# Where a recurrent block's scan states are emitted, its preparation in whole pieces, and a causal mask over one tile of keys

## The chip, the cores and the metric

The kernel runs on one core of a Trainium2 chip. The core has five engines that work side by side from queues of their own: TensorE (PE, matrix products; its weight loads are listed as PEld), VectorE (DVE), ScalarE (ACT, elementwise functions), GpSimd (POOL) and SyncE (SP, which issues the transfers). The metric is the device time of one execution in microseconds (us).

## The reference

The reference is a decoder of four layers over x of shape (4, 256, 256), that is 1024 tokens of width 256, with a context ctx_1024 of shape (4, 256, 128). Each layer has three parts, and each part is added and normalised, with a layernorm over the 256 features. The first five parts are the ones that matter here.

```python
x = _layernorm(x + _L0_attn_ref(x, ...))             # causal attention, 16 heads, one key/value head
x = _layernorm(x + _L0_xattn_ref(ctx_1024, x, ...))  # selective scan over the context, gated by x
x = _layernorm(x + _L0_ffn_ref(x, ...))              # "thought": 4 recurrent steps on the last token
x = _layernorm(x + _L1_attn_ref(x, ...))             # attention, 16 heads of 16, 4 key/value heads
x = _layernorm(x + _L1_xattn_ref(ctx_1024, x, ...))  # a second selective scan
...                                                  # experts and two more layers
```

The first attention masks keys above the diagonal before the softmax:

```python
sim = jnp.einsum('bhid,bjd->bhij', q, k)             # 16 heads of 128, rope on q and k
sim = jnp.where(jnp.triu(jnp.ones((n, n), dtype=bool), 1), neg, sim)
attn = jax.nn.softmax(sim - jnp.max(sim, axis=-1, keepdims=True), axis=-1)
```

The scans depend on the context alone, until the gate at their end:

```python
u = jax.nn.silu(xc + conv_b[None, :, None])          # xc: projection and 4-tap convolution
delta = jax.nn.softplus(jnp.einsum('er,brl->bel', dt_proj_w, dt_lo) + dt_proj_b[None, :, None])
dA = jnp.exp(d_t[..., None] * A)                     # 256 channels x 16 states
state = state * dA + (d_t * u_t)[..., None] * B_t[:, None, :]
y_t = jnp.einsum('ben,bn->be', state, C_t)
y = (y + D[None, :, None] * u) * jax.nn.silu(z)      # z is x
```

The thought's four steps form one dependent chain; what follows them covers all tokens:

```python
thought = x_norm[:, -1, :] @ agg_w + agg_b
for _ in range(4):
    t = jax.nn.gelu(layer_norm(thought, pn_gamma, pn_beta) @ d1_w + d1_b)
    thought = thought + (t @ d2_w + d2_b)
out = x + jax.nn.sigmoid(x @ gate_w + gate_b) * (thought @ bc_w + bc_b)[:, None, :]
return layer_norm(out, out_gamma, out_beta)
```

## The kernel before, in words

The 1024 tokens lie in 8 tiles of 128 partitions. x stays on the chip, with a transposed copy xT for the products. The parts run one after another; the two scans have no place of their own, but are pieces of work that other parts emit among their own instructions. Every helper of class `Core` (lines 45 to 215) issues one instruction: `K.mm` a matrix product (L132), `K.tt`, `K.ts`, `K.stt` on VectorE (L111 to L120), `K.ptt` on GpSimd (L123), `K.act` on ScalarE (L126), `K.reduce` a row maximum or sum on VectorE (L129). Most instructions therefore show the line of a helper and are told apart by their tiles. A scheduler puts each engine's instructions into an order of its own by priorities that follow the order of emission, so that the place where a piece of work is emitted moves it on the engines' queues, but does not fix it there.

**The first attention** (`run_mqa`, L232 to L395) loops over n from 0 to 31: batch n // 8, four heads, and tile t = n % 2 of that batch's two query tiles. The keys that such a tile may see are ns = 128 for even n and 256 for odd n. `queries` (L281) makes the rotated queries of two heads for a whole batch, one call for each n. `scores` (L297) fills one PSUM bank for two heads: a mask product in bf16 comes first and opens the accumulation (L307), then one f32 product for each head. The mask tile maskb is 256 wide, its first half zeros and its second the triangle; for odd n the mask product covers all 256 keys of both heads, 512 columns, of which the first 128 of each head add zeros. VectorE then takes the row maxima, ScalarE the exponentials p; `shares` scales them by the reciprocal sums, `turn` transposes them into pT, `sums` and `output` multiply by values and output weights. The first scan is begun ahead of the loop (`K.scans.begin("l0x")`), and every n emits two of its states (`K.scans.beside(2)`).

**A scan** (`Scans._steps`, L443) begins with a preparation. From the context it makes u (Silu), then delta and du: VectorE writes delta = product + bias (L481), ScalarE writes du = Abs of the same (L482), in four pieces of 512 each. Then softplus is put together as max(delta, 0) + Ln(1 + Exp(-|delta|)): Exp and Ln (L484 to L486) each run over the two channel chunks of 1024, and two VectorE operations for each chunk (L487 to L489) finish delta and du = delta times u. A state is one step of the loop over 4 batches and 16 states: SP's queue loads B and C for it into bc (256 KB, L515), ScalarE makes dA with two Exps, VectorE forms s = du times B, scans along the tokens (L522), multiplies by C, and two states later TensorE adds s into a PSUM bank (ssmps). bc and s have four buffers, dA three. `beside(n)` emits the next n states; a scan has 64.

**Thought** (`run_thought`, L645 to L788) begins the second scan (`K.scans.begin("l1x")`, L714) ahead of its four steps. A step is a chain: square, variance product, root on GpSimd, scale, the product with d1, Gelu, a transposition with the copy hT on ScalarE (L740), the product with d2, the copy add on ScalarE (L744) and the next ct. The gate's products fill in, and one Sigmoid makes all eight gates. After the fourth step thT is ready (L760), and there 24 states are emitted (L761). The tail follows: for each batch `gated` multiplies the gate by the broadcast thought and adds x, with moments on VectorE and a root on GpSimd; `added` normalises, adds and calls `settle`, which normalises again and transposes x into xT.

**The second attention** (`run_gqa`, from L997) makes query, key and value projections for 8 tiles, rotates them on VectorE and transposes them, with one state beside each tile, and then emits one state beside each of its 32 rounds: 24 + 8 + 32 are the second scan's 64 states.

Of the kernel before, what the change touches and what calls it, by code (L numbers as in the profile page):

```python
# [20 lines left out]
BF16 = mybir.dt.bfloat16  # L21
# [3 lines left out]
AF = mybir.ActivationFunctionType  # L25
# [6 lines left out]
P = 128  # L32
B, L, D = 4, 256, 256
NT = B * L // P
DC = D // P
# [170 lines left out]
def again(ap, n):  # L206

    return ap.unsqueeze(1).to_broadcast([ap.shape[0], n, ap.shape[1]])
# [23 lines left out]
def run_mqa(K, w, more):  # L232
    nc, tc = K.nc, K.tc
    with ExitStack() as ctx:
        one = ctx.enter_context(tc.tile_pool(name="mqa1", bufs=1))
# [7 lines left out]
        mask = one.tile([P, P], F32, name="mask")  # L243
# [2 lines left out]
            out=mask, in_=mask, compare_op=ALU.is_ge, fill=NEG, base=0, pattern=[[-1, P]], channel_multiplier=1  # L246
        )

        maskb = one.tile([P, 2 * P], BF16, name="maskb")
        nc.gpsimd.memset(maskb[:, 0:P], 0.0)  # L250
        nc.vector.tensor_copy(maskb[:, P : 2 * P], mask)
        rope = w["rope"]

        def rotated(out, ps, cos, sin):
# [9 lines left out]
        kT = one.tile([P, B * L], F32, name="kT")  # L264
# [32 lines left out]
        def scores(n):  # L297
            b, g, t = n // 8, n // 2 % 4, n % 2
            ns = P * (t + 1)
            p = wk.tile([P, 4, L], F32, name="p")  # L300
            nm = wk.tile([P, 4], F32, name="nm")
            sm = wk.tile([P, 4], F32, name="sm")
            for jj in range(2):
                q = qT[8 * b + 2 * g + jj]
                sc = psc.tile([P, 2, L], F32, name="sc", tag="sc")

                K.mm(sc[:, :, 0:ns], K.identb, again(maskb[:, 2 * P - ns :], 2), True, False)  # L307
                for j in range(2):
                    K.mm(sc[:, j, 0:ns], q[:, j, t * P : (t + 1) * P], kT[:, b * L : b * L + ns], False, j == 1)
                two = slice(2 * jj, 2 * jj + 2)  # L310
                K.reduce(nm[:, two], sc[:, :, 0:ns], MAX, negate=True)
                for j in range(2):
                    m = 2 * jj + j
                    K.act(p[:, m, 0:ns], sc[:, j, 0:ns], AF.Exp, bias=nm[:, m : m + 1], accum_out=sm[:, m : m + 1])
            made[n] = p, sm
# [46 lines left out]
        queries(1)  # L362
        values(0)
        scores(0)
        rest = [lambda: values(1), lambda: keys(1), lambda: values(2), lambda: values(3)]
        for n in (2, 3):
            queries(n)
        for n in range(N):
            shares(n)
            if n + 1 < N:  # L370
                scores(n + 1)
            if n + 4 < N:
                queries(n + 4)
            if n in (2, 3, 4, 5):
                rest.pop(0)()
            if n == 6:
                ready = ready_thought(K, more()) if K.fused(0) else iter(())
            if n > 9:
                next(ready, None)
            K.scans.beside(2)  # L380
            turn(n)
            if n:
                output(n - 1)
            sums(n)
            if n % 8 == 2 and n > 8 and K.fused(0):
                gate_pair(K, wk, y, n // 8 - 1)
# [12 lines left out]
class Scans:  # L399
# [43 lines left out]
    def _steps(self, pre):  # L443
        K, nc, w, wk = self.K, self.K.nc, self.w[pre], self.wk
# [4 lines left out]
        du = self.one.tile([P, DC, N], F32, name="du")  # L449
# [3 lines left out]
        for j in range(4):  # L453
            t = wk.tile([P, D], F32, name="tap", tag="bc", padded_shape=[P, 2 * L])
# [14 lines left out]
        for h in range(2):  # L469
# [8 lines left out]
            for c in range(DC):  # L478
# [2 lines left out]

                K.ts(delta[:, c, s], ps, cols[:, c, 1:2], None, ADD)  # L482
                K.act(du[:, c, s], ps, AF.Abs, bias=cols[:, c, 1:2])
        for func, kw in ((AF.Exp, dict(scale=-1.0)), (AF.Ln, dict(bias=K.eps[1.0]))):  # L484
            for c in range(DC):
                K.act(du[:, c, :], du[:, c, :], func, **kw)  # L486
        for c in range(DC):  # L487
            K.stt(delta[:, c, :], delta[:, c, :], 0.0, du[:, c, :], MAX, ADD)
            K.tt(du[:, c, :], delta[:, c, :], u[:, c, :], MUL)  # L489
# [18 lines left out]
        for b in range(B):  # L508
            lo = b * L
            for n in range(16):  # L510
# [3 lines left out]
                t = wk.tile([P, 2, L], F32, name="bc", tag="bc")  # L514
# [130 lines left out]
def run_thought(K, w, more):  # L645
    nc, tc = K.nc, K.tc
# [3 lines left out]
    with ExitStack() as ctx:  # L650
        one = ctx.enter_context(tc.tile_pool(name="th1", bufs=1))
# [106 lines left out]
        nc.vector.tensor_copy(mean, last)  # L758
        thT = wk.tile([P, DC, B], F32, name="thT")
        K.tt(thT, ct, again(mean, DC), ADD)  # L760
        K.scans.beside(24)  # L761

        def gated(b):

            ps = pm.tile([P, D], F32, name="ps", tag="mm")
            K.mm(ps, K.ident, row["bc_b"], True, False)
            for c in range(DC):
                K.mm(ps, thT[:, c, b : b + 1].to_broadcast([P, P]), w["bc"][:, c, :], False, c == DC - 1)
            for i in (2 * b, 2 * b + 1):
                K.tt(gate[:, i, :], gate[:, i, :], ps, MUL)  # L770
                K.tt(gate[:, i, :], gate[:, i, :], K.x[:, i, :], ADD)
                K.ptt(K.x[:, i, :], K.x[:, i, :], row["out_b"], ADD)
            return moments(gate[:, 2 * b : 2 * b + 2, :], P, 2)

        def added(b, mv, rstd):
            for t in range(2):
                i = 2 * b + t
                g = gate[:, i, :]
                K.stt(g, g, mv[:, t, 0:1], row["out_g"], SUB, MUL)
                K.stt(K.x[:, i, :], g, rstd[:, t : t + 1], K.x[:, i, :], MUL, ADD)  # L780
                K.settle(i)

        ahead = gated(0)
        for b in range(B):
            this = ahead
            if b + 1 < B:
                ahead = gated(b + 1)
            added(b, *this)  # L788

# [1441 lines left out]
def load_none(K, wp):  # L2233
    return {}


PARTS = [
    (load_mqa, run_mqa),
    (load_none, run_gate("l0x")),
    (load_thought, run_thought),  # L2240
    (load_gqa, run_gqa),
    (load_none, run_gate("l1x")),
# [210 lines left out]
```

## Time and profile before

| | |
|---|---|
| median of three runs | 2461.66 us (2461.66, 2462.14, 2454.41) |
| profiled execution, its own time | 2449.13 us |
| its span, first to last instruction | 2447.4 us |
| mean granted clock of TensorE | 0.952 |
| instructions | 28725 |
| PE busy | 2259.7 us (92%) |
| PEld busy | 1516.4 us (62%) |
| DVE busy | 1472.1 us (60%) |
| ACT busy | 808.9 us (33%) |
| POOL busy | 257.9 us (11%) |
| mask products | 64, of them 32 with 512 columns |
| scan states | 128, mean 1218 ns for the scan itself |

The profile is that of one execution. It gives, for each engine, the time busy; the span in 40 equal slices, where a digit is the busy share in tenths and PEclk the clock that the throttle granted to TensorE, in tenths of full speed; and groups of instructions. The trace behind it answers with timelines. A line of a timeline has the start and the duration in us, the engine, the line in the kernel, the operation, the tile written and the tiles read with their shapes, how many such instructions were folded into one line (x4), and in brackets the idle time ahead of it with the instruction that ended it. Neighbours on one engine overlap a little in these records, so that the distance between two starts is the better price of the first.

### The profile page before, as it was taken

Reading aid. Unit: us, or ns where it says so; the run is one execution under the profiler, and the core shown is the slowest. Engines: PE = TensorE matmul, PEld = TensorE weight load, DVE = VectorE, ACT = ScalarE, POOL = GpSimd, SP = SyncE. Lnnn points to the kernel's source line nnn. Section 1 sums busy time; section 2 is a strip of 40 time slices with the busy share of each in tenths; the row PEclk is TensorE's granted clock in tenths of the full one; section 3 lists DMA queues with packets and bytes.
Section 4 is the critical chain, followed back from the end, with each engine's and each line's share of the span. In section 5 each row is a group of like instructions: output and inputs, shape, how many; then the busy total and the mean of one; then the engine's idle time right before and its main releaser. Section 6 shows DMA issues by size and latency. Waiting matters only on the chain. (4 is left out here: it accounts for less than half of the span.)

```text
span 2447.4 us, 28725 instructions
## 1 busy us (share of the span) xinstructions
PE 2259.7 (92%) x10632; PEld 1516.4 (62%) x10632; DVE 1472.1 (60%) x3002; ACT 808.9 (33%) x1803; POOL 257.9 (11%) x422
## 2 busy tenths in 40 slices
PE   8899997769996999899999999999999988899997
PEld 4566763334433655537888888888776543476774
DVE  4899984989976121370465444454655676773566
ACT  5677665413441111261211111111113243343434
POOL 0000001030010322200110001100210003000001
PEclk9899998778988999999999999999989899999999
DMA  6222221412213644220131111110100002100000
GB/s 204 63 59 60 52 56 33 103 27 52 48 31 101 192 129 123 76 68 14 65 108 61 46 66 53 63 46 31 47 22 1 20 18 71 41 1 1 1 1 18
DMA packets 132834, 138.98 MB, mean 57 GB/s; under 512 B 13876, under 2 KB 120726, under 8 KB 130904
## 3 DMA queue, kind: packets, MB, share of 16 engines
q1 hardware_dynamic: 132696, 137.16, 19.5%
q8 instruction: 84, 1.38, 0.2%
q14 instruction: 54, 0.44, 0.1%
HBM read 134.27 MB, written 2.85 MB: 56 GB/s over the span
## 5 line engine op out<-in xcount | busy, mean ns | idle before, releaser
L132 PE MATMUL ps<-xw,xcT 128*128 128x256 f32 (+1 forms) x2304 | 518.9, 382 | 0.3 <-ACT YT L126 0.3
L132 PEld LDWEIGHTS ps<-xw,xcT 128*128 128x128 f32 x2304 | 430.8, 190 | 64.0 <-issue 1.9
L132 PE MATMUL sc<-kT,qT 32*128 32x256 f32 (+2 forms) x1024 | 240.4, 402 | 10.6 <-DVE qn L129 10.3
L132 PEld LDWEIGHTS sc<-kT,qT 128*128 128x128 f32 (+1 forms) x1024 | 152.0, 200 | 94.1 <-issue 59.5
L111 DVE TENSOR_TENSOR xp<-ps,xb 128x256 f32<-128x256 f32 x96 | 40.4, 421 | 231.7 <-PE ps L132 231.7
L126 ACT ACTIVATE dA<-delta,negA 128x255 f32<-128x255 f32 x256 | 119.0, 501 | 144.3 <-DVE s L522 142.7
L132 PE MATMUL ssmps<-s,idz 128*128 128x512 f32 x256 | 146.2, 680 | 16.5 <-DVE s L111 14.7
L522 DVE TENSOR_TENSOR_SCAN s<-dA,s 128x512 f32<-128x512 f32 x128 | 154.5, 1218 | 2.6
L111 DVE TENSOR_TENSOR hT<-u,a 128x512 f32<-128x512 f32 x48 | 33.1, 690 | 184.0 <-PE u L132 184.0
L126 ACT ACTIVATE p<-sc,nm 128x256 f32<-128x256 f32 (+1 forms) x256 | 111.9, 444 | 94.1 <-DVE nm L129 88.0
L126 ACT ACTIVATE sq<-xp 128x1024 f32<-128x1024 f32 x24 | 25.4, 1057 | 314.3 <-DVE xp L111 314.2
L132 PE MATMUL o<-pT,vt 128*128 128x256 f32 (+1 forms) x352 | 116.9, 453 | 9.8 <-ACT pT L332 9.4
L129 DVE TENSOR_REDUCE qn<-sc 128x2 f32<-128x480 f32 (+1 forms) x192 | 87.1, 506 | 40.5 <-PE sc L132 40.0
L169 POOL TENSOR_SCALAR rstd<-mv 128x2 f32<-128x2 f32 x48 | 11.6, 241 | 944.9 <-DVE mv L161 935.1
L126 ACT ACTIVATE e<-sT 128x512 f32<-128x512 f32 x128 | 70.9, 590 | 106.7 <-PE sT L132 105.6
L132 PE MATMUL sT<-q,kT 32*128 32x256 f32 (+1 forms) x384 | 101.5, 505 | 3.5 <-ACT e L126 3.3
L1489 DVE TENSOR_TENSOR_SCAN dec<-xT,idz 128x256 f32<-128x256 f32 (+1 forms) x192 | 89.8, 536 | 20.3 <-DMA xT<-ad 20.3
L129 DVE TENSOR_REDUCE nm<-sc 128x2 f32<-128x512 f32 (+1 forms) x128 | 77.3, 613 | 40.8 <-PE sc L132 40.3
L126 ACT ACTIVATE a<-g 128x512 f32<-128x512 f32 x48 | 28.8, 599 | 206.2 <-PE g L132 203.4
L132 PE MATMUL g<-xT,wj 128*128 128x512 f32 x192 | 90.3, 593 | 0.7 <-ACT rows L100 0.7
L132 PE MATMUL u<-xT,wj 128*128 128x512 f32 x192 | 90.4, 592 | 0.0
L111 DVE TENSOR_TENSOR s<-du,bc 128x512 f32<-128x512 f32 x128 | 87.6, 694 | 4.4 <-PE ssmps L132 2.4
(502 smaller groups left out, 3950.9 us busy)
## 6 DMA issues: line engine op xcount, KB each, us to landing
bc<-bcd SPq DMA_DIRECT2D x128, 256.0 KB, 4.5
xw<-in_l2a_xw_dram SPq DMA_DIRECT2D x24, 768.0 KB, 4.8
xT<-ad SPq DMA_DIRECT2D x12, 1024.0 KB, 4.5
wj<-in_l1f_gate_dram SPq DMA_DIRECT2D x48, 128.0 KB, 2.6
wj<-in_l1f_up_dram SPq DMA_DIRECT2D x48, 128.0 KB, 2.8
wj<-in_l1f_down_dram SPq DMA_DIRECT2D x48, 128.0 KB, 3.1
sel<-cwd SPq DMA_DIRECT2D x32, 192.0 KB, 3.2
sel<-cwd SPq DMA_DIRECT2D x32, 128.0 KB, 3.6
```

Of the source, the lines that this page charges most:

```text
L111: self.nc.vector.tensor_tensor(out=out, in0=a, in1=b, op=op)
L126: self.nc.scalar.activation(out, in_, func, **kw)
L129: self.nc.vector.tensor_reduce(out=out, in_=in_, axis=AX.X, op=op, **kw)
L132: self.nc.tensor.matmul(out, lhsT=lhsT, rhs=rhs, start=start, stop=stop)
L169: self.nc.gpsimd.tensor_scalar(out=out, in0=in_, scalar1=add, scalar2=None, op0=ADD)
L522: nc.vector.tensor_tensor_scan(out=s.rearrange("p c l -> p (c l)"), data0=dA.rearrange("p c l -> p (c l)"), data1=s.rearrange("p c l -> p ...
L1489: nc.vector.tensor_tensor_scan(out=dec[:, k, h, :], data0=ap[:, h, at(bb, k, j) : at(bb, k, 2)], data1=K.idz[:, 0 : (2 - j) * P], initial=0.0,
```

## The change

Three edits in three functions.

First, maskb is 128 wide and holds the triangle alone; the memset of its zero half is gone. In `scores` the two head products come first, the first of them opening the accumulation, and the mask product comes last and closes it. It covers the own tile's 128 keys of both heads, the last 128 of ns, so always 256 columns.

Second, the scan's Exp and Ln each run in one instruction over both chunks, 2048 wide. This holds for both scans.

Third, the 24 states that thought emitted between thT and its tail are emitted behind the tail, as the last statement of `run_thought`.

```diff
-        maskb = one.tile([P, 2 * P], BF16, name="maskb")
-        nc.gpsimd.memset(maskb[:, 0:P], 0.0)
-        nc.vector.tensor_copy(maskb[:, P : 2 * P], mask)
+        maskb = one.tile([P, P], BF16, name="maskb")
+        nc.vector.tensor_copy(maskb, mask)
...
-                K.mm(sc[:, :, 0:ns], K.identb, again(maskb[:, 2 * P - ns :], 2), True, False)
                 for j in range(2):
-                    K.mm(sc[:, j, 0:ns], q[:, j, t * P : (t + 1) * P], kT[:, b * L : b * L + ns], False, j == 1)
+                    K.mm(sc[:, j, 0:ns], q[:, j, t * P : (t + 1) * P], kT[:, b * L : b * L + ns], j == 0, False)
+                K.mm(sc[:, :, ns - P : ns], K.identb, again(maskb, 2), False, True)
...
-        for func, kw in ((AF.Exp, dict(scale=-1.0)), (AF.Ln, dict(bias=K.eps[1.0]))):
-            for c in range(DC):
-                K.act(du[:, c, :], du[:, c, :], func, **kw)
+        K.act(du, du, AF.Exp, scale=-1.0)
+        K.act(du, du, AF.Ln, bias=K.eps[1.0])
...
         thT = wk.tile([P, DC, B], F32, name="thT")
         K.tt(thT, ct, again(mean, DC), ADD)
-        K.scans.beside(24)
...
             added(b, *this)
+
+        K.scans.beside(24)
```

## The prediction

> **What bounds the kernel now.** I read the page's busy slices first, then a table of busy time by stretch, then the timelines of TensorE, ScalarE and VectorE where the change acts, and last the order of both programs' instructions on each engine. A slice is 61 us.
>
> ```profile
> PE   8899997769996999899999999999999988899997
> DVE  4899984989976121370465444454655676773566
> PEclk9899998778988999999999999999989899999999
> ```
>
> All three edits act in the first 10 slices: first attention with the first scan (to about 370 us), thought with the second scan's preparation (to 513), second attention's preparation. VectorE is near its limit there and TensorE's clock sags in slices 7 to 9. From the second attention's first maxima on (about 545 us) both programs have the same order on every engine, so what is gained before is carried to the end unchanged.
>
> ```profile
> 175.00:200.00 25.00, 25.00 (x114) 18.24 (x112) 24.08 (x38) 16.01 (x47) 0.00 (x0) 1.00 0.29 56
> 275.00:300.00 25.00, 25.00 (x112) 18.43 (x111) 22.95 (x37) 16.39 (x50) 0.00 (x0) 1.00 0.29 64
> 480.00:500.00 20.00, 8.84 (x16) 3.60 (x16) 18.58 (x52) 2.33 (x6) 8.74 (x15) 0.61 0.23 52
> 500.00:520.00 20.00, 9.04 (x23) 5.22 (x24) 15.94 (x44) 3.09 (x7) 7.12 (x14) 0.53 0.07 15
> 560.00:580.00 20.00, 19.35 (x60) 10.48 (x58) 18.01 (x27) 7.00 (x16) 0.00 (x0) 0.58 0.18 43
> ```
>
> After the stretch and its length stand PE, weight loads, DVE, ACT, POOL, then the granted clock. In the first attention's steady part TensorE has no gap, so TensorE sets the pace: two query tiles take 17.5 us (275.02 to 292.53). In the thought's end VectorE is the busiest and TensorE half idle at a sagging clock.
>
> **The mask.** From TensorE's timeline, start and duration:
>
> ```profile
> 283.65 0.27 PE L132 MATMUL sc<-maskb,identb 128*128 128x256 bf16 x1
> 283.76 0.61 PE L132 MATMUL sc<-kT,qT 128*128 128x128 f32 x4
> ...
> 292.53 0.38 PE L132 MATMUL sc<-maskb,identb 128*128 128x512 bf16 x1
> 292.74 1.03 PE L132 MATMUL sc<-kT,qT 128*128 128x256 f32 x4
> ```
>
> Durations overlap, so I take the distance of starts: 0.21 us for the 512-column mask, 0.11 for the 256-column one. 32 of the 64 masks (odd n) shrink from 512 to 256: 32 x 0.105 = 3.4 us at most. Only where TensorE has no gap does that reach the end; the stretches 175 to 225, 250 to 300 and 325 to 350 are full, which is some 8 odd tiles: 8 x 2 x 0.105 = 1.7. Against it: at the start a mask matmul could run in TensorE's idle time ahead of the query's rope (one stood at 11.99, where TensorE then waited 2.53); behind the heads it no longer can, +0.2. The POOL memset of 0.20 at 2.2 us lies under the loads: nothing, and 0.2 if that cover is gone. I take **-1.5** (bounds -3.4 to +0.2).
>
> **One-piece Exp and Ln.** ScalarE's timeline in the thought:
>
> ```profile
> 408.14 1.06 ACT L126 ACTIVATE du<-du 128x1024 f32<-128x1024 f32 x1
> 409.10 0.67 ACT L126 ACTIVATE du<-ssmps,w_l1x_cols 128x512 f32<-128x512 f32 x1
> 409.79 1.28 ACT L126 ACT_TABLE_LOAD   x1
> 411.08 1.15 ACT L126 ACTIVATE du<-du,eps 128x1024 f32<-128x1024 f32 x1
> 412.25 1.28 ACT L126 ACT_TABLE_LOAD   x1
> 413.55 1.06 ACT L126 ACTIVATE du<-du 128x1024 f32<-128x1024 f32 x1
> 414.51 0.35 ACT L740 COPY hT<-ps 128x256 f32<-128x256 f32 x1
> 414.88 1.28 ACT L126 ACT_TABLE_LOAD   x1
> 416.17 1.15 ACT L126 ACTIVATE du<-du,eps 128x1024 f32<-128x1024 f32 x1
> ```
>
> Before, chunk 0's Exp and Ln run between the chunks' Abs, so the table changes Exp, Ln, Exp, Ln. In one piece nothing can begin before the last Abs (ends 409.77), but there is one change fewer. Here a rule of the Trainium skill ("ScalarE: Activation LUTs", What ACT_TABLE_LOAD costs) differs from the rows: it adds about 1.38 us of drain to the load's 1.283, 2.66 a switch. The rows show the load at 409.79 and the next ACTIVATE at 411.08: 1.29 and no drain visible. Over both scans four loads go: 5.2 us of ScalarE by the row, 10.6 by the rule. I take the row, and of it only what the chain shows.
>
> A 2048-wide piece is not in the trace with these functions; the 2048-wide Sigmoid took 1.91 and 1024 more elements cost 0.85, so Exp 1.91, Ln 2.0. Thought: 409.8 + load 1.28 + Exp 1.91 + a copy 0.38 + load 1.28 + Ln 2.0 = 416.65, against 417.32 before. But VectorE had finished chunk 0's two operations under chunk 1's functions; now all four (4.9 us) follow: 421.6 against 419.84, so the first state is **1.7 us late**. In exchange the thought's own first step gets ScalarE earlier: the copy into hT stood ready at about 408 and ran at 414.51 behind those blocks, so the steps come about 6 us earlier at best. If the scheduler's order doesn't give that, 1.7 late is all that is left.
>
> First attention: VectorE waited 1.67 (72.75) and 2.48 us (78.89) for these pieces, the first state's product began at 82.61. After: last Abs 73.3, two pT copies 0.94, Exp 1.9, load 1.29, Ln 2.0: 79.4; four VectorE operations 4.9 and a key rope now ahead 0.6: 84.9; less 2.8 of rope work that has moved into the waits: 82.1. So **-0.5** (bounds -2 to +3: all the waits' 4.15 half filled, or the rope work not moved).
>
> **The 24 states behind the thought.** By the orders, 24 of the second scan's states stood ahead of the tail on VectorE, 13 do now; 11 move behind the tail and ahead of the second attention's first rope. Their count, their 256 KB loads on SP's queue, their two Exps on ScalarE and their product on TensorE stay; on SP the router's load is passed from behind 24 to behind 11 of them, and nothing before the experts reads it. A state is 2.32 us of VectorE: 25.5 us for the eleven.
>
> Before the tail: VectorE idles 6.9 us between 419.87 and 484.13 (single waits of 0.2 to 1.6, the longest 1.59 for a load of B and C). With the steps about 6 us earlier and 11 states fewer to wait under, I put the rest at 2.2: -4.7 + 1.7 late = **-3.0** (bounds -4.6 and +1.7).
>
> ```profile
> 483.00 1.22 DVE L522 TENSOR_TENSOR_SCAN s<-dA,s 128x512 f32<-128x512 f32 x1
> 484.13 0.40 DVE L111 TENSOR_TENSOR gate<-gate,ps 128x256 f32<-128x256 f32 x1
> ...
> 512.09 0.73 DVE L117 TENSOR_SCALAR x<-x,mv,rstd 128x256 f32<-128x256 f32 x2 [0.91 <-POOL rstd L123]
> ...
> 517.49 1.02 DVE L111 TENSOR_TENSOR t<-ps,w_l1a_rope 128x160 f32<-128x160 f32 x4 [0.63 <-PE ps L132]
> ...
> 519.43 1.02 DVE L111 TENSOR_TENSOR t<-ps,w_l1a_rope 128x160 f32<-128x160 f32 x4 [0.79 <-PE ps L132]
> ...
> 521.16 0.69 DVE L98 COPY qT<-ps 128x512 f32<-128x512 f32 x1 [0.58 <-PE ps L802]
> ```
>
> The tail (484.13 to 512.8) keeps its operations and POOL waits: 0. Behind it VectorE waited for the second attention's first projections, 0.63 + 0.79 + 0.58, and 0.91 before that; with 11 states between, TensorE makes the projections of tiles 0 to 2 under 25.5 us of VectorE work: 0.63 + 0.79 + 0.58 + 0.6 = **-2.6**. Two later waits, 2.54 (538.31) and 1.59 (550.38), could go with them: -6.7. Against it the cover has a price at a low clock: a state's product takes 2.08 us there (1.02 to 1.12 at full clock), a projection matmul 0.69 (0.40): 11 x 2.08 + 12 x 0.69 = 31.2, or 5.7 more than the states cover.
>
> Here a rule speaks against the change: "TensorE: Matmul & The Clock Gate" (The HAM clock gate) says that the clock halves after an idle window of about 3.4 us and comes back after about as much unbroken work. The tail has four such gaps on TensorE (6.35, 4.90, 5.55, 3.28), and the rows show 0.61 and 0.53 there; by the rule alone the stretch behind it is cold, +5.7. But the row at 560 to 580 shows 0.58 with TensorE busy 19.35 of 20, so the granted clock is not idle gaps alone, and 465 to 484, the states alone, had 0.68. I take the warm value.
>
> **The sum.** -1.5 - 0.5 - 3.0 - 2.6 = -7.6. The profiled execution took 2449.13 us (span 2447.4, 1.7 around it): 2441.5 after. It lies 12.5 below the median of the runs, 2461.66; with the same distance **2454.1**, -0.31%. About 0.3%, 7.4 us, is what a measurement of this kernel can tell from no change.
>
> **Rivals.** *Neutral, 2460.* VectorE's work between 410 and 545 us is the same in sum, so moved states only move waits; the mask's 1.5 is all that passes. For it: 18.58 of 20 and 19.24 of 20 (445 to 465) are near full. Against it: the named waits on TensorE at 517 to 521 have work to fill them.
>
> *More, 2447.* The waits of 2.54 and 1.59 vanish (4.1), the load wait 1.6 too, and the attention's preparation gives its other 1.5: -7.6 - 7.2 = -14.8. For it: TensorE is three tiles ahead when VectorE comes to the ropes. Against it: TensorE is busy 19.33 of 20 from 520 to 540 and now carries 11 more products there.
>
> *Slower, 2471.* The second attention's preparation is TensorE's, and those 11 products arrive with a sagging clock: one more 20-us stretch at 0.58 as at 560 to 580 does 11.6 us of full-clock work, 8.4 late. From one such stretch on the gain of 7.6 is gone; two make 2461.7 - 7.6 + 16.8 = 2470.9. For it: 11 products x 1.02 is more work where TensorE has 0.7 idle. Against it: the tail's colder stretch is followed by 0.83 and 1.00 within 20 and 40 us, and part of that work now falls under states.
>
> *The move doesn't happen:* the program orders by its own priorities, and 13 of the states remain ahead of the tail; the orders show 11 moved, so this is excluded in full and counted already in part.
>
> **How the numbers follow.** Likeliest 0.43, own range 2448 to 2460; neutral 0.14; more 0.16; slower 0.27. Faster by over 0.3% means below 2454.3: half of the likeliest (0.22), and more (0.16), with a little of the slower case's near end: 0.39. Slower, above 2469: most of the slower case and a bit for the preparation's bounds adding up: 0.25. Same: 0.36. The range leaves out less than 0.1 on each side: below, the case "more" with the mask's other 1.9 and the preparation's bound (2443); above, two cold stretches and the preparation's +3 (2473).
>
> **What would show it.** Right: masks of 128x256 only and 0.11 apart behind the heads; two table loads fewer per scan; the tail's first gate product 28 to 32 us earlier, at about 453; no wait on TensorE at the second attention's first three ropes, and its first maxima some 8 us earlier. Wrong: the first state of the second scan later than 422 with hT still behind Ln; a granted clock below 0.6 for more than 20 us between the tail and 600; new waits of VectorE for the products' buffers while TensorE is full.

## The result and the profile after

The changed kernel takes 2447.78 us in the median, from 2442.51 to 2459.49, against 2456.98 for the kernel before over as many executions (2448.87 to 2469.99). The ratio is 0.9961 with a 95% interval of [0.9945, 0.9977]: 9.6 us faster, with 5.7 to 13.5 us in the interval. The forecast sum was -7.6. The forecast time, 2454.1, lies higher than the measured one partly because its starting point, 2461.66, was the median of three executions; 2456.98 less 7.6 would have been 2449.4.

By the time alone the result lies just below the likeliest case's own range (2448 to 2460) and near the case "more" (2447); which of the two it was is read from the stages below.

The two profiled executions show little of the gain: their spans are 2447.4 and 2446.5. Where the difference went is told in the last section.

The page of the kernel after, busy slices:

```profile
PE   7889998689987999899999999999999988899997
DVE  4899984998875121371465444454655676773566
PEclk9999998787987999999999999999989899999999
```

Slice 7 of TensorE (counted from 0, 428 to 489 us) fell from 7 to 6 and slice 8 rose from 6 to 8, because the thought's tail now lies in the one and the moved states with the next projections in the other. From slice 13 on TensorE's row is the same digit for digit.

The kernel after, busy time by stretch (after the length PE, weight loads, DVE, ACT, POOL, granted clock):

```profile
175.00:200.00 25.00, 21.63 (x94) 15.11 (x94) 24.10 (x38) 16.14 (x47) 0.00 (x0) 1.00 0.22 53
275.00:300.00 25.00, 25.00 (x111) 17.93 (x110) 23.06 (x36) 16.91 (x51) 0.00 (x0) 1.00 0.26 62
480.00:500.00 20.00, 14.97 (x35) 6.88 (x36) 19.09 (x33) 6.03 (x13) 1.28 (x2) 0.82 0.36 79
500.00:520.00 20.00, 14.44 (x35) 5.41 (x34) 20.00 (x38) 7.25 (x18) 6.48 (x12) 0.83 0.43 105
560.00:580.00 20.00, 20.00 (x77) 9.72 (x76) 17.76 (x26) 7.20 (x16) 0.00 (x0) 0.52 0.28 58
```

Between 480 and 520 VectorE is full now, 39.1 of 40 us where it was 34.5, and TensorE's clock is 0.82 and 0.83 instead of 0.61 and 0.53. The work in these two stretches is not the same: the tail, and the low clock with it, has moved ahead to 463 to 487 (see the part on the clock). At 560 to 580 little changed: TensorE full and the clock near half.

The kernel after, TensorE's timeline in the first attention:

```profile
284.50 0.61 PE L132 MATMUL sc<-kT,qT 128*128 128x128 f32 x4
284.95 0.27 PE L132 MATMUL sc<-maskb,identb 128*128 128x256 bf16 x1
...
293.38 1.03 PE L132 MATMUL sc<-kT,qT 128*128 128x256 f32 x4
294.24 0.27 PE L132 MATMUL sc<-maskb,identb 128*128 128x256 bf16 x1
294.35 1.03 PE L132 MATMUL sc<-kT,qT 128*128 128x256 f32 x4
```

Every mask product is 256 wide and takes 0.11 from start to start, as said.

To read executions stage by stage I take four marks from VectorE's and TensorE's timelines: the first convolution product of the first scan, the 64th row maximum of the first attention, the end of the second scan's last du operation, and the 17th row maximum of the second attention. A is from the first to the second mark, B to the third, C to the fourth. The idle time is the sum of VectorE's gaps over 0.1 us in C.

| kernel | A | B | C | B + C | idle in C |
|---|---|---|---|---|---|
| before | 318.69 | 69.99 | 139.54 | 209.53 | 17.9 |
| after | 316.83 | 72.69 | 131.60 | 204.29 | 10.7 |
| mask alone | 318.05 | 70.00 | 139.49 | 209.49 | 17.9 |
| one-piece Exp and Ln alone | 318.29 | 72.64 | 135.13 | 207.77 | 13.9 |
| states moved alone | 318.77 | 71.38 | 136.95 | 208.33 | 15.5 |
| mask's place alone | 321.48 | 69.99 | 139.69 | 209.68 | 18.1 |
| after, states put back | 316.77 | 71.28 | 135.41 | 206.69 | 14.2 |
| after, two pieces again | 318.26 | 69.98 | 134.79 | 204.77 | 13.5 |
| after, states in the tail | 316.72 | 72.63 | 131.94 | 204.57 | 10.7 |
| after, one projection bank | 316.69 | 72.62 | 132.59 | 205.21 | 10.6 |
| after, mask dose | 330.24 | 72.65 | 131.67 | 204.32 | 10.8 |
| after, scan begun early | 316.83 | 68.90 | 132.20 | 201.10 | 10.9 |
| early, and three banks | 316.17 | 59.92 | 139.60 | 199.52 | 17.1 |

Up to du the changed kernel, the one with the states put back, the one with the states in the tail and the one with one projection bank have the same order on every engine. Their A agrees within 0.2 us (316.69 to 316.83), which is how far a difference in A can be trusted where no longer half-clock window falls into one of the two.

C less its idle time is 121 to 122.5 us in every row. VectorE has that much work between du and the 17th maximum whatever the order, and what an edit gains in C is the idle time that it takes away.

### The profile page after: what moved, and what is told of

Read it like the earlier page. It is cut to its first block, busy times and chain, and to the rows that moved or that the text cites. A ratio compares the mean times of both kernels' runs of the same rounds, so it can differ in the third digit from the quotient of the medians.

```text
span 2446.5 us, 28718 instructions
## 1 busy us (share of the span) xinstructions
PE 2259.3 (92%) x10632; PEld 1518.1 (62%) x10632; DVE 1472.0 (60%) x3002; ACT 803.3 (33%) x1795; POOL 260.5 (11%) x421
## 5 line engine op out<-in xcount | busy, mean ns | idle before, releaser
L132 PEld LDWEIGHTS ssmps<-s,idz 128*128 128x128 f32 x256 | 47.8, 208 | 74.4 <-DVE s L111 40.5
```

What stands on the lines that cost most here:

```text
L132: self.nc.tensor.matmul(out, lhsT=lhsT, rhs=rhs, start=start, stop=stop)
```

## The experiments

### The mask alone

```diff
-                K.mm(sc[:, :, 0:ns], K.identb, again(maskb[:, 2 * P - ns :], 2), True, False)
                 for j in range(2):
-                    K.mm(sc[:, j, 0:ns], q[:, j, t * P : (t + 1) * P], kT[:, b * L : b * L + ns], False, j == 1)
+                    K.mm(sc[:, j, 0:ns], q[:, j, t * P : (t + 1) * P], kT[:, b * L : b * L + ns], j == 0, False)
+                K.mm(sc[:, :, ns - P : ns], K.identb, again(maskb, 2), False, True)
```

> Only the mask edit (tile of 128, mask product behind the heads, 256 columns). The prediction's theory: TensorE passes on half of the 3.4 us that 32 narrower products save; from the first row maximum to the 64th 1.5 us less than the 330.3 of before, nothing after that, median -1.5 (ratio 0.9994). Rival A, all of it passes: from the first scan to the 64th maximum 3.4 less, as in the changed kernel (262.7 for 266.0), ratio 0.9986. Rival B, VectorE sets the pace there: 0.

Ratio 0.9998, interval [0.9978, 1.0018]. A is 0.6 us shorter, of 3.4 that the products save, and nothing follows in B and C. From the first scan to the 64th maximum it takes 264.77 for 266.03. Rival A (all 3.4) is out in this kernel. The row maxima of the first attention tell where the 0.6 lies. The 13th comes 80.87 us after the first convolution product for 80.85; from there to the 43rd it takes 146.56 for 146.61; from the 43rd to the 64th 90.62 for 91.23. In the steady part narrower products gain nothing, which is rival B; the whole gain lies behind the 43rd maximum.

### The mask's place alone

```diff
-                K.mm(sc[:, :, 0:ns], K.identb, again(maskb[:, 2 * P - ns :], 2), True, False)
...
+                K.mm(sc[:, :, 0:ns], K.identb, again(maskb[:, 2 * P - ns :], 2), False, True)
```

> Only the place of the mask product: behind the two heads, still 256 wide tile and 512 columns for odd n. The prediction's theory: the width is what saves, so the first attention's 330.3 us stay within 0.5, ratio 1.000. Rival, the order of the products is what helps (the products of a pair close together, mask no longer ahead of the ropes): -1.5 or more with the widths unchanged. Rival, it costs at the start: +0.5.

Ratio 1.001, interval [0.9985, 1.0035]. A is 2.8 longer in this execution, outside what the theory and its rivals gave. By the row maxima 0.4 of it is there at the 13th, which is about what the rival "it costs at the start" gave. Nothing is added up to the 40th, and 2.4 come between the 40th and the 46th. There the clock differs. The busy time from the 40th to the 43rd maximum of the kernel before, and then of this one:

```profile
238.16:258.62 20.46, 17.33 (x80) 12.05 (x79) 19.48 (x37) 14.02 (x38) 0.93 (x2) 1.00 0.21 60
```

```profile
240.97:263.10 22.13, 19.30 (x77) 13.76 (x76) 19.68 (x36) 14.02 (x38) 0.93 (x2) 0.85 0.23 55
```

A mean of 0.85 over 22.1 us is 6.8 us at half. So most of the 2.8 goes with the clock of this one execution and not with the place. The place shows no gain.

### Three more mask products

```diff
+                for _ in range(3):
+                    K.mm(sc[:, :, ns - P : ns], K.identb, again(zerob, 2), False, False)
                 K.mm(sc[:, :, ns - P : ns], K.identb, again(maskb, 2), False, True)
```

> The changed kernel with three more mask products of zeros over the own tile's keys in front of each real one: 192 more of 256 columns, at 0.11 us 20 us of TensorE work in the first attention, output unchanged. The prediction's theory, that about half of TensorE's time there reaches the end: +10 us from the first scan to the 64th maximum. Rival A, TensorE sets the pace throughout: +20. Rival B, VectorE sets it: under +4.

Ratio to the kernel before 1.0021, interval [1.0002, 1.0041]; the median, 2462.71, is 14.9 above that of the changed kernel. From the first scan to the 64th maximum it takes 277.69 for 262.69, +15.0, and A is 13.4 longer: two thirds to three quarters of the 20 us are passed on, more than the half of the theory and less than rival A. The busy time from the 13th to the 40th row maximum, of the kernel before, the changed kernel and this one:

```profile
112.01:238.16 126.15, 120.81 (x540) 85.15 (x539) 121.37 (x206) 90.80 (x260) 5.33 (x8) 0.99 0.27 58
```

```profile
113.20:239.39 126.19, 117.12 (x534) 82.20 (x533) 121.41 (x207) 90.76 (x260) 5.34 (x8) 1.00 0.26 58
```

```profile
112.65:244.63 131.98, 127.83 (x620) 93.07 (x619) 124.39 (x207) 91.38 (x258) 5.35 (x8) 0.99 0.26 57
```

With narrower products TensorE's busy time fell by 3.7 us (part of that is clock), and the stretch is as long as before; VectorE is busy 121.4 us of it in both. The 78 products added in this stretch, 8.5 us at 0.109, lengthen it by 5.8. The price of a product upwards is not its price downwards. That VectorE sets the pace once TensorE has a little less to do fits these rows; no run took work from VectorE to show it.

### Exp and Ln in one piece alone

```diff
-        for func, kw in ((AF.Exp, dict(scale=-1.0)), (AF.Ln, dict(bias=K.eps[1.0]))):
-            for c in range(DC):
-                K.act(du[:, c, :], du[:, c, :], func, **kw)
+        K.act(du, du, AF.Exp, scale=-1.0)
+        K.act(du, du, AF.Ln, bias=K.eps[1.0])
```

> Only Exp and Ln in one piece, both scans. The prediction's theory: first attention -0.5; in the thought VectorE finishes du 1.7 to 2.7 us later after the 64th maximum (before: 70.0), and part of it comes back because the thought's chain has its ScalarE copies earlier: VectorE's idle between du and thT falls from 5.9 to about 3.1 as in the changed kernel, net 0 +- 1 at the second attention's first maxima; ratio 1.000. Rival, the edit is what helps the thought: net -2 or more there. Rival, it costs its lateness in full: +2.7, ratio 1.001.

Ratio 0.9981, interval [0.9965, 0.9998], the only single edit whose interval excludes no change. A is 0.4 shorter (0.8 at the 13th row maximum). In the thought du is done 2.6 later after the 64th maximum (B), and C is 4.4 shorter: net -1.8 at the 17th maximum, close to the rival that the edit helps the thought by 2. At the first row maximum it was -1.7 (176.03 for 177.69).

### The states moved alone

```diff
         K.tt(thT, ct, again(mean, DC), ADD)
-        K.scans.beside(24)
...
             added(b, *this)
+
+        K.scans.beside(24)
```

> Only the 24 states behind the tail. The prediction's theory: the time up to du is unchanged, the tail's first gate product is some 27 us earlier (484 to 457), VectorE has no wait on TensorE at the first three ropes, and from du to the 17th maximum of the second attention it takes 3 to 5 us less than 139.5; ratio 0.998 to 0.999. Rival, moved states only move waits: 0 within 1 us, ratio 1.000. Rival, TensorE is cold: waits on ssmps and ps behind the tail, +3 or more.

Ratio 0.9993, interval [0.9976, 1.0011]. The tail's first gate product comes at 460.21, 24 us earlier, there is no wait at the first three ropes, and the second attention's first maximum comes 2.9 us sooner after the 64th of the first. Then 1.7 are lost again, and 1.2 remain. VectorE's timeline of this kernel:

```profile
543.24 0.69 DVE L98 COPY qT<-ps 128x512 f32<-128x512 f32 x1 [4.31 <-PE ps L803]
```

and TensorE's, ahead of it:

```profile
531.50 2.07 PE L132 MATMUL sc<-kT,qT 32*128 32x256 f32 x4
533.50 2.08 PE L132 MATMUL ssmps<-s,idz 128*128 128x512 f32 x2
535.50 2.07 PE L132 MATMUL sc<-kT,qT 32*128 32x256 f32 x4
537.50 2.08 PE L132 MATMUL ssmps<-s,idz 128*128 128x512 f32 x2
539.37 1.49 PE L132 MATMUL ps<-w_l1a_wqkv,xT 128*128 128x384 f32 x2
```

Four score products take 2.07 there, where at full clock (TensorE's timeline of the changed kernel, 526.83) four took 1.13. This is the slower rival's mechanism at work: the preparation met a half-clock stretch of 13.7 us. Whether that belongs to the move is what the next run asks.

### After, with Exp and Ln in two pieces again

```diff
-        K.act(du, du, AF.Exp, scale=-1.0)
-        K.act(du, du, AF.Ln, bias=K.eps[1.0])
+        for func, kw in ((AF.Exp, dict(scale=-1.0)), (AF.Ln, dict(bias=K.eps[1.0]))):
+            for c in range(DC):
+                K.act(du[:, c, :], du[:, c, :], func, **kw)
```

> The changed kernel with Exp and Ln in two pieces again (mask and move stay). The move alone had a wait of 4.3 us on the projections at 538.9, with the clock at half from 530 to 542. Theory 1, that wait was the place of the half-clock windows in that execution: here 205 to 206.5 us from the 64th maximum of the first attention to the 17th of the second, ratio 0.998. Theory 2, the one-piece edit makes the move worth more: 208.3 again, with a wait over 3 us on the projections, ratio 0.999 or above.

Ratio 0.9994, interval [0.9969, 1.0019]. B + C is 204.77, so theory 1: with the same order behind the first attention as the moved states alone, C is 2.2 us shorter and the wait in question is this one, from VectorE's timeline of this kernel:

```profile
538.02 0.69 DVE L98 COPY qT<-ps 128x512 f32<-128x512 f32 x1 [1.31 <-PE ps L802]
```

The granted clock was 0.66 in the ten microseconds from 528, against 0.50 in the ten from 530 with the move alone. The remaining 1.4 of the difference lies in B, where the move alone had a clock of 0.83 in the ten microseconds from 386 and this kernel 1.00. So the move by itself is worth 4.8 us in this execution, with 6.8 us at half clock behind 528, and 1.2 in the one with 13.7 us there and a window in B. Both are single executions; that the clock makes the whole difference is inferred from where it lies.

### After, with the states put back

```diff
         K.tt(thT, ct, again(mean, DC), ADD)
+        K.scans.beside(24)
...
-        K.scans.beside(24)
```

> The changed kernel with the 24 states put back ahead of the tail (mask and one-piece Exp and Ln stay). From the 64th maximum of the first attention to the 17th row maximum of the second attention: before 209.5, changed 204.3, one-piece alone 207.8, move alone 208.3 us. The theory now, parts nearly independent and each worth the VectorE idle time that it removes: as the one-piece kernel, 207.8 +- 0.7, the first attention as the changed kernel (316.8 from the first convolution product to the 64th maximum); ratio to before 0.998. Rival, the parts are worth something only together: 209.5 and ratio 1.000.

Ratio 0.9993, interval [0.9972, 1.0014], which alone would allow both theories. B + C is 206.69, a little better than expected, and A is as short as the changed kernel's. With a clock of 1.00 from 386 to 396, du is done 71.28 us after the 64th maximum: the one-piece edit costs 1.3 us there, and the 72.6 to 72.7 of five other kernels, with 0.83 to 0.85 in that place, hold 1.4 of clock. The parts are nearly independent: -2.8 for the one piece and -4.8 for the move make -7.6; the changed kernel has -5.2 in its execution, -6.6 if that 1.4 is put aside, which leaves 1 us that the parts do not give together.

### After, with the states in the tail

```diff
             added(b, *this)
-
-        K.scans.beside(24)
+            K.scans.beside(6)
```

> The changed kernel, but the 24 states emitted six at a time behind each batch of the tail. By the idle theory they can fill the four waits on the root (0.84, 0.84, 0.91, 0.91, 3.5 us in all with small ones) of the tail: 2 to 3 us less up to the second attention's 17th maximum than the changed kernel's 204.3. Rival, the states push the tail's dependent steps and with them the transpositions and projections back: 204 or more, and waits on TensorE at the first ropes again.

Ratio 0.9973, interval [0.9957, 0.9989]. B + C is 204.57, no better. The scheduler put the states as a block behind the third batch, and VectorE's four waits on the root are all still there (0.83, 0.91, 0.91, 0.91): the rival's number, though not by its mechanism, since no wait on TensorE came back. Whether states inside those waits would gain stays untried.

### After, with one bank for the projections

```diff
-        pm = early.enter_context(tc.tile_pool(name="gqap", bufs=3, space=PSUM))
+        pm = early.enter_context(tc.tile_pool(name="gqap", bufs=1, space=PSUM))
```

> The changed kernel with one PSUM bank instead of three for the second attention's projections, so that TensorE cannot work ahead on tiles 1 and 2 while the moved states run. The prediction's theory (the moved states cover TensorE's projections, 2.6 us, because those lie ready in three banks): waits on TensorE at each of the first ropes come back, and from the 64th maximum to the second attention's first row maximum it takes 2 us or more longer than 172.5. Rival, the gain there comes from the order of VectorE's work alone: within 1 us of 172.5.

Ratio 0.9945, interval [0.9923, 0.9966], not slower than the changed kernel. The wait came back, in VectorE's timeline of this kernel:

```profile
515.68 0.33 DVE L111 TENSOR_TENSOR t<-ps,w_l1a_rope 128x160 f32<-128x160 f32 x1 [3.63 <-PE ps L132]
```

and to the second attention's first maximum it takes 177.14 for 172.52, 4.6 more. So the projections lying ready in three banks is what the cover consists of. But behind it VectorE waits no more: between the first and the 17th maximum its idle time fell from 4.1 to 0, and at the 17th only 0.9 is left. A wait removed at the ropes was paid for 20 us later in the changed kernel, and the other way round here. The cover decides where VectorE waits, then, and only 0.9 of what it removes reaches the 17th maximum; the move keeps the rest of its gain without it.

### The second scan begun at the top of thought

```diff
+        K.scans.begin("l1x")
         d1, d2, d1b = w["d1"], w["d2"], w["d1b"]
...
-        K.scans.begin("l1x")
```

> The changed kernel with the second scan begun at the top of thought, ahead of its first layernorm, not behind it. If the end of the preparation sets when VectorE gets busy (it idles about 40 of the 70 us between the 64th maximum and du), each us that the preparation ends earlier is a us gained: du 8 to 12 us earlier, ratio to before 0.992. Rival, the preparation's own chain through one PSUM bank sets it: du 0 to 4 us earlier, ratio 0.995 to 0.996 like the changed kernel.

Ratio 0.9963, interval [0.9946, 0.998]. du is done 3.8 us earlier after the 64th maximum, the rival's 0 to 4 (1.4 of it can be the clock, 1.00 here from 386 to 396 for 0.83), and C is 0.6 longer than the changed kernel's, so that 3.2 of it is kept at the 17th maximum. In the times the gain over the changed kernel is not shown.

### The early begin, and more banks for the preparation

```diff
+    def either(self):
+        self.flip = not self.flip
+        if self.flip:
+            return self.bank()
+        return self.K.tp.tile([P, 512], F32, name="ps", tag="tp")
...
-                ps = self.bank()
+                ps = self.either()
```

The exchange at the end of the diff is made at all three places of the preparation: convolution, xp and dt.

> The same early begin, and the preparation's products (convolution, xp, dt) alternate between its own PSUM bank and the two banks for transpositions, in both scans. If the single bank is what stretches the preparation, both ends of it come earlier: the first scan's first state 10 us or more earlier, du of the second 15 us or more earlier than in the changed kernel, ratio to before 0.985 or less. Rival, the transpositions then wait for those banks and the attention and the thought's chain lose what the scan gains: ratio 0.995 or above.

Ratio 0.9941, interval [0.9923, 0.9958], the lowest of all; its interval overlaps with the changed kernel's, so that a gain over it is likely and not shown by the times. Both theories hold a part. The first scan's first state comes at 45.8 us after the first convolution product for 54.1, and du 12.8 us earlier in B. But the attention and the thought pay: the first attention's ninth row maximum comes 21.6 us later after that product (59.2 for 37.6), so that A ends only 0.7 sooner, and the thought's first hT comes at 416.5 for 397.1. C has 17.1 us of idle time again. What is won is 4.8 us in B + C.

## Why the prediction was right, and where not

**The total.** The interval holds the -7.6. By stages the changed kernel has -1.9 in A and -5.2 in B + C, -7.1 in all; the prediction had -2.0 for the first attention and -5.6 for the thought and what follows. What the times show beyond that, 2.5 us, lies within the interval, and no stage of the profile carries it. That the first attention's two terms come so near to their sum is luck: the mask gave less, and what made up for it is 1.3 us in the scan's preparation that was reckoned otherwise. Against the case "more" stand the two later waits, which did not go. One forecast of size was missed: the second attention's first maximum comes 5.2 us sooner after the 64th of the first (172.52 for 177.69), not some 8.

**The mask, -1.5.** Alone it gave -0.6 in A. The step "TensorE has no gap, so TensorE sets the pace" failed. It was read from stretches chosen because TensorE is full in them; over the steady part as a whole, from the 13th to the 40th maximum, VectorE is as busy (121.37 of 126.15 us) as TensorE (120.81), and there the narrower products gained nothing: 126.15 before, 126.11 with the mask alone, 126.19 changed. The share of the path holds for work added (two thirds) and not for work taken away. The +0.2 at the start came as reckoned: the 7th row maximum is 0.2 later with the mask alone and in the changed kernel.

**One piece in the first attention, -0.5.** Alone it gave -0.8 by the 13th maximum and -0.4 in all of A, with a half-clock window between the 40th and the 46th, where 0.4 were lost; together with the mask the 13th maximum comes 1.3 sooner. The way there was not the forecast one. In the changed kernel the first state's product comes 52.9 us after the first convolution product for 51.5 before, so 1.5 later and not 0.5 sooner, and the row maxima are ahead all the same. The changed kernel's -1.9 in A is then 1.3 up to the 13th maximum, nothing in the steady part and 0.6 behind the 43rd.

**One piece in the thought: 1.7 late and six early.** The lateness was 1.3. Six us came on ScalarE and not at the end of the step. ScalarE's, VectorE's and TensorE's timelines of the kernel after:

```profile
411.74 1.28 ACT L126 ACT_TABLE_LOAD   x1
413.03 1.91 ACT L126 ACTIVATE du<-du 128x2048 f32<-128x2048 f32 x1
414.85 0.36 ACT L742 COPY add<-ps 128x257 f32<-128x257 f32 x1
415.22 1.28 ACT L126 ACT_TABLE_LOAD   x1
416.51 2.00 ACT L126 ACTIVATE du<-du,eps 128x2048 f32<-128x2048 f32 x1
```

```profile
418.55 2.36 DVE L120 SCALAR_TENSOR_TENSOR delta<-delta,du 128x1024 f32<-128x1024 f32 x2 [6.65 <-ACT du L126]
420.82 2.35 DVE L111 TENSOR_TENSOR du<-delta,u 128x1024 f32<-128x1024 f32 x2
423.10 0.15 DVE L115 TENSOR_SCALAR rstd<-ps 128x4 f32<-128x4 f32 x1
```

```profile
418.63 1.02 PE L132 MATMUL ps<-sq,over 128*128 128x4 f32 x4 [2.16 <-ACT sq L126]
```

VectorE's timeline of the kernel before, and of the changed one with the states put back, at the same variance:

```profile
423.80 0.16 DVE L115 TENSOR_SCALAR rstd<-ps 128x4 f32<-128x4 f32 x1 [1.43 <-PE ps L132]
```

```profile
421.52 0.15 DVE L115 TENSOR_SCALAR rstd<-ps 128x4 f32<-128x4 f32 x1
```

The durations were as estimated, 1.91 and 2.00, and the change of table took 1.29 from its start to the next piece's, as in the trace before. The copy into hT ran at 410.61, 3.9 us earlier than before, and the variance product at 418.63, 4.1 earlier. But its rstd is an operation on VectorE, and there it stood behind all four du operations: 423.10, only 0.7 earlier than before. With the states put back, where no half-clock window meets the thought's start, the same chain can be read from the 64th maximum on: the copy into hT comes after 58.7 us for 64.7, the full 6 us earlier, the rstd after 71.2 for 74.0, and thT after 99.7 for 104.3. The step of the prediction that failed is "the steps come about 6 us earlier": it followed the chain on ScalarE and did not ask what stood ahead of it on VectorE. What came in its place is 2.8 at the first rstd and 4.6 at thT (2.0 in the changed kernel, with its half-clock window). The rstd was ready when the du operations ended, so that VectorE's wait of 1.43 that stood there before is gone, and the waits up to the tail fell from 6.9 to 3.1 us in the changed kernel (to 2.5 with the states put back). The -3.0 for this part was nearly met, with the cause half wrong: the one piece and not the move brings it. With the states put back B + C is still 2.8 shorter than before.

**The move, -2.6 behind the tail.** The waits of 0.63, 0.79 and 0.58 are gone, and the tail's own idle time fell by 0.6 (4.1 to 3.5), though a wait of 0.91 still stands at its end. VectorE's timeline of the kernel after:

```profile
456.32 0.73 DVE L111 TENSOR_TENSOR gate<-gate,ps 128x256 f32<-128x256 f32 x2
...
483.42 0.73 DVE L117 TENSOR_SCALAR x<-x,mv,rstd 128x256 f32<-128x256 f32 x2 [0.91 <-POOL rstd L123]
...
509.25 0.31 DVE L111 TENSOR_TENSOR t<-ps,w_l1a_rope 128x160 f32<-128x160 f32 x1
```

The tail's first gate product comes 27.8 us earlier (484.13 to 456.32), at the near edge of the 28 to 32 that were forecast; between 484 and 523 VectorE has no gap over 0.1 us. The later waits of 2.54 and 1.59 did not go: they are 1.31, 0.92 and 1.84, so the case "more" is out. The 2.6 is right as a sum of waits, and the reason given for it is right in part: with one projection bank the ropes wait again, and yet only 0.9 is lost at the 17th maximum.

**The clock.** The warm value was the right one: 0.82 and 0.83 behind the tail. The busy time in the tail's half-clock stretch, of the kernel before and of the kernel after:

```profile
491.40:518.70 27.30, 8.96 (x23) 5.14 (x24) 22.82 (x66) 2.88 (x6) 10.73 (x19) 0.50 0.04 9
```

```profile
463.40:487.10 23.70, 8.13 (x21) 4.35 (x22) 20.20 (x60) 1.17 (x2) 9.79 (x17) 0.50 0.11 17
```

The cold stretch belongs to the tail and moved with it. In all 13 kernels the half clock begins 7.0 to 9.1 us after the tail's first gate product, 2.4 to 5.0 us into TensorE's first long gap there (5.2 to 7.8 us long; 6.35 before, 7.16 after). In these two the clock is full again 6.1 and 4.6 us after TensorE's last gap of over 1 us. That agrees with the rule of the Trainium skill that was weighed ("TensorE: Matmul & The Clock Gate", The HAM clock gate). What the prediction had wrong was its use of it: it let the rule keep the stretch behind the tail cold, where TensorE works again without long gaps. What did come there, in the moved states alone, was a half-clock stretch while TensorE had no gap, which the rule does not give. So the slower rival was wrong in its sign for the changed kernel and right in its mechanism: in that run it took 2.2 us of C and 1.4 of B. The 16.8 us that the rival reckoned with were met in none.

Two of the signs of being wrong came, in part. The first state comes later than 422 (423.21), but hT did not stand behind Ln. The clock was at half for 23.9 us between the tail and 600, from 555.5 on; the kernel before had 20.5 us of it from 563.1 on, so that this sign did not separate the two.

## What to carry to other kernels

Where one engine has work enough for a whole stretch, sum its idle time there before and after: the length followed that sum within 2 us in all 13 kernels, while single waits came, went and moved. Follow a dependent chain across every engine that it visits, and ask on each what the same edit has put ahead of it: most of 4 us won on ScalarE and TensorE were given back in one VectorE queue. Compare the engines' busy time over the whole of a steady part, not in stretches where one of them is full. Price work that is taken away by the engine that is next to the limit, not by the share that added work would pass on.

## What the runs showed of the hardware

The granted clock falls to half in two ways. One goes with TensorE's gaps, as in the tail. The other is short windows while TensorE is busy, which came in some executions and not in others with the same instructions. One of these in B: the busy time by stretch of the moved states alone, and then of the changed kernel with two pieces again:

```profile
386.00:396.00 10.00, 10.00 (x56) 5.68 (x54) 1.58 (x7) 3.36 (x5) 1.02 (x1) 0.83 0.01 2
```

```profile
386.00:396.00 10.00, 9.85 (x58) 5.46 (x57) 1.49 (x7) 4.88 (x6) 1.02 (x1) 1.00 0.04 9
```

A mean of 0.83 over 10 us is 3.4 us at half, the length of the window that the Trainium skill names ("TensorE: Matmul & The Clock Gate", The HAM clock gate). Of the eleven kernels that begin the second scan at the same place six had it (0.83 to 0.85; with the mask dose 11 us later, where everything is) and five did not. Two pairs have the same order on every engine up to du, and in each only one execution had the window: du came 72.69 us after the 64th maximum in the changed kernel and 71.28 with the states put back, 71.38 with the states moved alone and 69.99 in the kernel before. So the window costs 1.4 us of the thought's chain. TensorE was busy 9.4 to 10 of the 10 us in both groups, so that no gap in these 10 us called it.

In one long stretch far behind the change, from 1807 to 2137, the code of all kernels is the same. The busy time there, of the kernel before, of Exp and Ln in one piece alone, of the mask alone and of the moved states alone:

```profile
1807.00:2137.00 330.00, 292.55 (x1536) 163.93 (x1537) 223.63 (x544) 106.97 (x195) 35.30 (x45) 0.92 0.10 32
```

```profile
1807.00:2137.00 330.00, 293.33 (x1563) 164.57 (x1563) 227.39 (x553) 107.94 (x198) 35.75 (x47) 0.93 0.10 32
```

```profile
1807.00:2137.00 330.00, 294.98 (x1516) 162.87 (x1510) 217.05 (x528) 102.50 (x179) 35.30 (x45) 0.89 0.10 32
```

```profile
1807.00:2137.00 330.00, 296.87 (x1505) 163.13 (x1504) 211.83 (x517) 99.10 (x174) 35.69 (x47) 0.87 0.10 32
```

The clocks 0.93, 0.92, 0.89 and 0.87 go with spans of 2444.6, 2447.4, 2454.1 and 2461.9 us: from the first row maximum of a later attention to that of the one after it, some 322 us apart, it took 318.3, 322.3, 328.9 and 335.0 us. That is most of the difference between these four spans, and none of it is the change. The profiled pair lost its difference elsewhere, in three places. At the start the changed kernel's first convolution product came 2.5 us later (33.66 for 31.16), with a clock of 0.89 for 1.00 from 5 to 20; with one projection bank, the same order there, it came at 31.13. It was 4.9 us ahead when the experts began, then took 358.0 for 354.9 up to the next part's first projection, with a clock of 0.82 for 0.89 from 760 to 780, and 1.1 more up to 1807.

The longest half-clock stretch with TensorE full, in the kernel after:

```profile
555.60:579.30 23.70, 23.70 (x87) 12.78 (x89) 21.57 (x31) 8.25 (x19) 0.00 (x0) 0.50 0.25 51
```

So half clock does not come with gaps alone. In ten of the 13 kernels a stretch of this kind, 20.5 or 23.9 us long, begins between 550 and 567, in the second attention's rounds, so that its place goes with the work. Why TensorE gets half clock there, and what decides where the short windows fall, was not found.
